# Placing batch 0's turning transfers behind the loads of the beginning, with a new load order and new deadlines

## The chip, the cores and the metric

The kernel runs on one core of one Trainium2 chip. The metric is the device time of one execution in microseconds (us). A core has five engines that each work through their own instructions in order: TensorE (PE in the profile; its weight loads are listed as PEld), VectorE (DVE), ScalarE (ACT), GpSimd (POOL) and SyncE (SP). SP issues every transfer (DMA) of this kernel, so its queue is the queue of all loads, turning transfers and stores. Engines wait for one another by semaphores.

## The reference, cut to what matters

There are B = 4 batches of S = 256 rows of H = 512 values. Four layers follow one another:

```python
# L0: a mixture of low-rank updates; ctx (4, 64, 512) plays the part of lora_A
w     = softmax(x @ router_W.T + router_b)            # (4, 256, 8)
a_sum = einsum('bsh,arh->bsr', x, ctx)               # sums over a, the batches of ctx
x     = nan_to_num(x + 0.5 * einsum('bsn,bsnh->bsh', w, einsum('bsr,nhr->bsnh', a_sum, lora_B)))
# L1: cross attention to ctx, 32 heads of 16, masked, then layer norm
Q, K, V = x @ Wq.T + bq, ctx @ Wk.T + bk, ctx @ Wv.T + bv
x     = layernorm(x + attention(Q, K, V, mask) @ Wo.T + bo) * ln_g + ln_b
# L2 and L3, the same function with the same weights: 4 blocks each
idx   = the 8 nearest of 512 columns of ctx[b] for each column (squared distance over 64 rows)
for i in range(4):
    p = leaky_relu(x)                                # x seen as (256, 512) per batch
    x = (f[i] @ p + sum over the 8 neighbours of f[i] @ p[:, idx]) / 9 + x
```

Each batch's chain goes through L0, L1 and then eight blocks, each of which needs the one before. The neighbour search depends on ctx alone and is needed only when the batch's first block begins.

## The kernel before, in words

For every batch the kernel builds the operations of `mixture` (L0; `mix` does it for each half of 128 rows), `values`, `queries` and `attention` (L1), `nearest` (the search) and eight times `block`. `keys`, `masks` and `lora_a` are made once for all batches.

**The search.** `nearest(b)` computes on PE four PSUM banks `dist` of negated half distances for batch b: `cross` (line 517) and the squares (line 530). For each bank j, DVE finds the eight largest values (`top`, line 537) and replaces them by a mark (`rest`, line 540), ACT makes zeros and ones of it (`near`, line 547, bf16), and POOL adds the identity (line 556). Then SP issues a DMA that transposes `near` into a quarter of the tile `turned` (line 566): this is what is called a turning transfer here, and there are four per batch. ACT last copies `turned` into the four `nbr` tiles of the batch (line 580), which the blocks multiply by on PE (line 920): there the sum over neighbours is a matmul.

**Batch 0's chain at the beginning.** `route` on PE (line 396), a small softmax on DVE and `z` (line 424), zT on PE (442) and its copy on ACT (447), `upd` on PE (452), x on DVE (467), then `hi` and `lo` (473, 474) on DVE, their sum on POOL (475), `odd` (476) and the predicated copy (477) on DVE, which are nan_to_num; then x1T on PE (481), its copy on ACT (487), and q on PE (690). Line 850 is the addition of attention's output to x, also on DVE.

**The planner.** No order is written out by hand. Every operation is added to a `Plan` with its engine, a cost in us, and the keys that it reads and writes. `emit` then simulates the engines: it always takes, for each engine, among the ready operations that could start first the one of lowest rank, and emits the earliest of these choices. So it fixes the order of the instructions on each engine, and the choice of tiles; it is no wait on the chip. The chip waits only for what the tiles demand: data, places, and a free DMA semaphore. An operation's rank is its batch's entry in `DEADLINES` less the costs behind it; a load's rank is its place in the list of loads, ahead of everything else. A load ends, for the planner, at the latest landing so far plus its size over `RATE` (0.3 MB per us), and at most `LANES` = 8 loads are under way:

```python
if op.load:
    op.end = max(op.end + 1.4, self.landed[-1]) + op.load / RATE
    self.landed.append(op.end)
op.end += op.lag
```

A turning transfer has no size: it costs SP the time `TURN` and lands `LAG` later by the planner's reckoning, whatever loads are under way.

**Places.** Tiles of a kind share a few places that the planner hands out: 8 PSUM banks, of which `stage` may hold 7 (blocks take a bank without `stage`), 5 of `half` (sq, rest, hi, lo, zTs, kT, seen and others), 5 of `near`, 4 of `full` (z, qT, turned, p), 3 of `xT` (xT and x1T). A tile can be written only when the operations on its place's last holder are done.

The functions that the diff touches:

Of the kernel before, what the change touches and what calls it, by code (L numbers as in the profile page):

```python
# [17 lines left out]
B, S, H = 4, 256, 512  # L18
# [10 lines left out]
SLOPE = 0.01  # L29
LN_EPS = 1e-5  # L30
LOW = -3.0e38
DEADLINES = (0.0, 2.0, 12.0, 17.0)

# [5 lines left out]
WARM = 20  # L41
LANES = 8
RATE = 0.3
TURN, LAG = 1.2, 1.2


class Buf:
# [121 lines left out]
def xattn_seq_kernel(ctx: ExitStack, tc: tile.TileContext, a: dict, out: bass.AP):  # L169
# [10 lines left out]
    shapes = {  # L180
        "bank": (psum, [128, 512], F32, 8),
        "xT": (keep, [128, NC, S], F32, 3),
        "s": (work, [128, H], F32, 8),
        "pT": (work, [128, H], F32, 4),
        "half": (work, [128, H], F32, 5),
        "full": (work, [128, 2, H], F32, 4),
        "wp": (work, [128, 2 * S], F32R, 8),
        "near": (work, [128, H], BF16, 5),
# [5 lines left out]
        pool, shape, dtype, _ = shapes[kind]  # L194
        return pool.tile(shape, dtype, tag=f"{kind}{place}", name=name)

    plan = Plan({kind: n for kind, (_, _, _, n) in shapes.items()} | {"stage": 7}, make)
    pe, act, dve, pool = (
        lambda *args, _e=e, **kw: plan.add(_e, *args, **kw) for e in ("PE", "ACT", "DVE", "POOL")
    )  # L200
# [9 lines left out]
    cxx = [keep.tile([128, H], F32, name=f"cxx{b}") for b in range(B)]  # L210
# [10 lines left out]
    rw = keep.tile([128, NC, NB + R], F32, name="rw")  # L221
    fT = keep.tile([128, NBLK, S // 128, S], F32, name="fT")
# [29 lines left out]
    def load(key, mb, dst, src, after=()):  # L252
        loads.append(key)
        plan.add("SP", 0.45, lambda: S_.dma_start(out=dst(), in_=src), after, (key,), rank=len(loads) - 1e4, load=mb)
# [4 lines left out]
    def load_xT(b):  # L259

        after = (("x1T", 1, 0),) if b == B - 1 else ()
        load(xT[b], 0.5, lambda: xT[b].tile.rearrange("p c t -> p (c t)"), a["xT"][b], after)

    def load_x(b):
        load(("x", b), 0.5, lambda: x1[b].rearrange("p l h -> p (l h)"), a["x"][b])

    def load_w(n):
        load(n, 1.0, lambda: w[n].rearrange("p c o -> p (c o)"), a[n])

    def load_k(o):  # L270
        load(("WkT", o), 0.25, lambda: WkT[o], a["WkT"][:, bass.ts(o, H)])

    def load_points(b):
        load(("cxx", b), 0.13, lambda: cxx[b][0:64], a["ctx"][b])
# [3 lines left out]
    load_k(0)  # L278
    load("ctxT", 0.5, lambda: ctxT.rearrange("p c b v -> p (c b v)"), a["ctxT"])
    load("small", 0.05, lambda: consts, a["small"])  # L280
    load_k(1)
    load_points(1)
    load_xT(0)
    load_w("lora_BT")
    load_k(3)
    load_points(2)
    load_x(0)
    load_k(2)
    load_points(3)
    load_w("WqT")  # L290
    load("mask_i", 0.12, lambda: mask_i.rearrange("p b v -> p (b v)"), a["mask"].partition_broadcast(128))
    load("rows1", 0.5, lambda: rows1, a["rows1"].partition_broadcast(128))
    load_w("WvT")
    load_xT(1)
    load("rows2", 0.5, lambda: rows2, a["rows2"].partition_broadcast(128))
    load_x(1)
    load_w("WoT")
    load_x(2)
    load("fT", 1.0, lambda: fT.rearrange("p i c o -> p (i c o)"), a["fsideT"])
    load_xT(2)  # L300


    dve(0.15, lambda: V_.memset(ones, 1.0), (), ("ones",))
# [192 lines left out]
    def nearest(b):  # L496
        sq = Buf("half", f"sq{b}")
        if b:
            act(0.6, lambda: A_.copy(cxx[b][64:128], cxx[b][0:64]), (("cxx", b),), (("cxx2", b),))
        act(0.6, lambda: A_.activation(sq.tile[0:64], cxx[b][0:64], AF.Square), (("cxx", b),), (sq,))  # L500
        act(0.6, lambda: A_.copy(csq[b][0:64], sq.tile[0:64]), (sq,), (("csq", b),))
        (pool if b else dve)(
            1.15 if b else 0.69,
            lambda: (G_ if b else V_).tensor_tensor(csq[b][64:128], sq.tile[0:64], csq[b][0:64].bitcast(F32), ALU.subtract),
            (sq, ("csq", b)),
            (("csq2", b),),
        )
        turned = Buf("full", f"turned{b}")
        dist = [Buf("bank", f"d2_{b}_{j}", "stage") for j in range(H // 128)]


        for k in range(2):

            def cross(k=k):
                for j in (2 * k, 2 * k + 1):
                    r = slice(64 * (j % 2), 64 * (j % 2) + 64)
                    T_.matmul(
                        dist[j].tile,
                        lhsT=cxx[b][r, bass.ts(j, 128)],
                        rhs=cxx[b][r],  # L520
                        start=True,
                        stop=False,
                        tile_position=(64 * (j % 2), 0),
                    )

            pe(0.9, cross, (("cxx", b), ("cxx2", b)), (dist[2 * k], dist[2 * k + 1], ("d2", b, k)))
            for j in (2 * k, 2 * k + 1):
                pe(
                    0.24,
                    lambda j=j: T_.matmul(dist[j].tile, lhsT=mhalf_r, rhs=csq[b], start=False, stop=True),  # L530
                    (("csq", b), ("csq2", b), "mhalf_r"),
                    (dist[j], ("d2", b, 2 + j)),
                )
        for j in range(H // 128):
            ps, top = dist[j], Buf("small", f"top{b}_{j}")
            rest, near = Buf("half", f"rest{b}_{j}"), Buf("near", f"near{b}_{j}")
            dve(0.69, lambda ps=ps, top=top: V_.max(top.tile[:, 0:KNN], ps.tile), (ps,), (top,))
            dve(
                0.76,
                lambda ps=ps, top=top, rest=rest: V_.match_replace(rest.tile, top.tile[:, 0:KNN], ps.tile, LOW),  # L540
                (ps, top),
                (rest,),
            )

            act(
                0.62,
                lambda rest=rest, near=near: A_.activation(
                    near.tile, rest.tile, AF.Relu, bias=above, scale=-(2.0**-123)
                ),
                (rest, "above"),  # L550
                (near,),
            )

            pool(
                0.3,
                lambda j=j, near=near: G_.tensor_tensor(
                    near.tile[:, bass.ts(j, 128)], near.tile[:, bass.ts(j, 128)], ident_h, ALU.add
                ),
                ("ident_h",),
                (near,),  # L560
            )

            plan.add(
                "SP",
                TURN,
                lambda j=j, near=near: S_.dma_start_transpose(
                    out=turned.tile.rearrange("p l h -> p (l h)").bitcast(BF16).rearrange("p (k n) -> p k n", k=4)[
                        :, :, bass.ts(j, 128)
                    ],
                    in_=near.tile,  # L570
                ),
                (near, turned),
                (("turned", b, j),),
                lag=LAG,
            )
        for k in range(H // 128):

            def store(k=k):
                nbr[b, k] = keep.tile([128, H], F32R, tag=nbr_tag[b][k], name=f"nbr{b}_{k}")
                A_.copy(  # L580
                    nbr[b, k],
                    turned.tile.rearrange("p l h -> p (l h)").bitcast(BF16)[:, bass.ts(k, H)],
                )


            gone = [("kT", o) for o in range(NC)] if b == 1 else []
            if b > 1:
                gone = [("d2", i, j) for i in (2 * b - 4, 2 * b - 3) for j in range(2 + H // 128)]
            act(0.6, store, (turned, *(("turned", b, j) for j in range(H // 128)), *gone), (("nbr", b, k),))
# [359 lines left out]
    for b in range(B):  # L949
        plan.batch = b  # L950
        if b == B - 1:
            load_xT(b)
            load_x(b)
        mixture(b)
        values(b)
        queries(b)
        nearest(b)
        for i in range(2 * NBLK):
            plan.unit = (b, i)
            block(b, i)  # L960
        plan.unit = None
    plan.emit(DEADLINES)

# [48 lines left out]
```

## Time and profile before

| what | us |
|---|---|
| median of three runs | 409.84 (409.74 to 410.01) |
| the profiled execution, its own time | 411.24 |
| its span, from the first to the last instruction | 408.9 |
| granted TensorE clock, mean | 0.994 of full |

The page divides the span into 40 equal slices of 10.2 us; each digit is the busy share of a slice in tenths:

```profile
PE   8996999999799999999999999999999999999995
DVE  4629669699889999873776554646455464635443
ACT  3823534335478574341223111111111111111110
DMA  6999410000020000000001000000000000010102
GB/s 200 353 349 334 105 52 2 0 2 2 0 53 2 0 2 2 0 2 0 2 0 26 2 0 0 2 0 2 0 1 2 0 0 2 0 51 2 51 0 103
```

The first four slices hold the loads. The first block begins at 145.8 us (line 889); from about 205 us on PE does nothing but blocks. A row of the timeline gives start, duration, engine, line, operation, tiles, shape and count, and in brackets the idle time of that engine before it and what ended it. In SP's timeline the first transfers that turn stand among the loads:

```profile
17.26 1.30 SPq L566 DMA_TRANSPOSE turned<-near  x1
18.61 0.57 SPq L254 DMA_DIRECT2D rows<-in_rows  x1
19.22 0.43 SPq L254 DMA_DIRECT2D x<-in_x  x1
20.71 0.33 SPq L254 DMA_DIRECT2D WoT<-in_WoT  x1
21.15 9.35 SPq L566 DMA_TRANSPOSE turned<-near  x3
30.55 0.57 SPq L254 DMA_DIRECT2D x<-in_x  x1
31.17 0.44 SPq L254 DMA_DIRECT2D fT<-in_fsideT  x1
31.71 1.38 SPq L566 DMA_TRANSPOSE turned<-near  x1
```

The four at 17.26 and 21.15 are batch 0's.

### The profile page before, as it was taken

The numbers are of one execution on the slowest core, as the hardware profiler recorded it, in microseconds if no ns is written. First come the engines' busy times: TensorE is split into PE (matmuls) and PEld (weight loads), VectorE is DVE, ScalarE is ACT, GpSimd is POOL, SyncE is SP. The second block draws the span as 40 slices with busy tenths as digits, with TensorE's granted clock in tenths as the row PEclk, the third lists the DMA queues.
The fourth block names the chain that finished last, engine by engine and source line by source line (L and its number), as shares of the span: only waits on it lengthen the run. The fifth ranks groups of instructions, "written<-read, shape, count | busy, mean of one in ns | idle before, by whom it ended". The sixth has DMA issues, their size and how long they took to land.

```text
span 408.9 us, 5691 instructions
## 1 busy us (share of the span) xinstructions
PE 394.7 (97%) x2244; PEld 302.9 (74%) x2244; DVE 266.0 (65%) x476; ACT 132.0 (32%) x236; POOL 100.3 (25%) x110
## 2 busy tenths in 40 slices
PE   8996999999799999999999999999999999999995
PEld 5753598646676686766878888888888888888884
DVE  4629669699889999873776554646455464635443
ACT  3823534335478574341223111111111111111110
POOL 4854240326736690950500000000000000000000
PEclk9999999999899999999999999999999999999999
DMA  6999410000020000000001000000000000010102
GB/s 200 353 349 334 105 52 2 0 2 2 0 53 2 0 2 2 0 2 0 2 0 26 2 0 0 2 0 2 0 1 2 0 0 2 0 51 2 51 0 103
DMA packets 13450, 17.42 MB, mean 43 GB/s; under 512 B 9392, under 2 KB 9520, under 8 KB 12784
## 3 DMA queue, kind: packets, MB, share of 16 engines
q1 hardware_dynamic: 13424, 17.07, 13.5%
q8 instruction: 17, 0.28, 0.3%
q14 instruction: 9, 0.07, 0.1%
HBM read 12.87 MB, written 2.10 MB: 37 GB/s over the span
## 4 chain that ended last, share of the span: by engine, by line
PE 76%; DVE 14%; DMA 4%; ACT 2%; POOL 2%; issue 1%; SPq 0%; DVEq 0%; ACTq 0%; POOLq 0%
PE blk L920 29%; PE wp L889 26%; PE q L690 6%; PE upd L452 5%; PE o L838 3%; DMA turned<-near 3%; PE pT L806 2%; DVE den L772 2%; PE s L731 1%; DVE x L477 1%; DMA ctxT<-in_ctxT 1%; DVE s L763 1%; DVE odd L476 1%; DVE mx L757 1%; DVE p L877 1%
## 5 line engine op out<-in xcount | busy, mean ns | idle before, releaser
L889 PE MATMUL wp<-fT,p 128*128 128x256 f32 x512 | 120.3, 379 | 0.0
L920 PE MATMUL blk<-nbr,wph 128*128 128x512 f32 x256 | 112.1, 438 | 0.0
L889 PEld LDWEIGHTS wp<-fT,p 128*128 128x128 f32 x512 | 96.5, 189 | 16.5 <-issue 1.4
L905 DVE TENSOR_TENSOR wpl<-wp,wph 128x512 fp32r<-128x512 f32 x64 | 44.2, 690 | 93.5 <-ACT wph L902 93.5
L920 PE MATMUL blk<-nbr,wpl 128*128 128x512 f32 x256 | 100.5, 392 | 0.1
L902 ACT CAST wph<-wp 128x512 fp32r<-128x512 f32 x64 | 37.5, 586 | 177.7 <-PE wp L889 177.7
L920 PEld LDWEIGHTS blk<-nbr,wph 128*128 128x128 f32 x256 | 48.2, 188 | 11.4 <-issue 1.2
L920 PEld LDWEIGHTS blk<-nbr,wpl 128*128 128x128 f32 x256 | 48.2, 188 | 10.3 <-DVE wpl L905 0.4
L932 DVE SCALAR_TENSOR_TENSOR x<-blk,x 128x512 f32<-128x512 f32 x64 | 42.6, 686 | 11.0 <-PE blk L920 11.0
L877 DVE SCALAR_TENSOR_TENSOR p<-x 128x512 f32<-128x512 f32 x64 | 44.9, 736 | 2.5 <-POOL x L864 1.9
L794 POOL TENSOR_TENSOR s<-s,rden 128x512 f32<-128x512 f32 x32 | 35.9, 1152 | 37.7 <-DVE rden L784 24.4
L690 PE MATMUL q<-x1T,WqT 128*128 128x256 f32 x128 | 30.8, 393 | 2.4 <-DVE x L850 2.4
L838 PE MATMUL o<-WoT,avTs 128*128 128x512 f32 x64 | 30.1, 600 | 0.5 <-ACT avTs L832 0.4
L690 PEld LDWEIGHTS q<-x1T,WqT 128*128 128x128 f32 x128 | 24.3, 195 | 6.8 <-DVE x L850 2.6
L452 PE MATMUL upd<-lora_BT,zTs 128*128 128x512 f32 x64 | 28.7, 595 | 0.0
L757 DVE TENSOR_REDUCE mx<-s 128x8 f32<-128x512 f32 x32 | 19.9, 682 | 7.7 <-PE s L731 7.7
L769 ACT ACTIVATE s<-s 128x512 f32<-128x512 f32 x32 | 18.8, 626 | 14.4 <-DVE s L763 14.4
L452 PEld LDWEIGHTS upd<-lora_BT,zTs 128*128 128x128 f32 x64 | 11.9, 190 | 12.8 <-issue 11.7
L772 DVE TENSOR_REDUCE den<-s 128x8 f32<-128x512 f32 x32 | 20.1, 675 | 0.8 <-ACT s L769 0.8
L811 ACT COPY pTs<-pT 128x512 f32<-128x512 f32 x32 | 17.2, 590 | 9.0 <-PE pT L806 9.0
L763 DVE TENSOR_TENSOR s<-s,mx 128x512 f32<-128x512 f32 x32 | 19.9, 679 | 0.0
L838 PEld LDWEIGHTS o<-WoT,avTs 128*128 128x128 f32 x64 | 11.4, 190 | 11.2 <-issue 9.7
(94 smaller groups left out, 370.5 us busy)
## 6 DMA issues: line engine op xcount, KB each, us to landing
xT<-in_xT SPq DMA_DIRECT2D x4, 512.0 KB, 7.1
x<-in_x SPq DMA_DIRECT2D x4, 512.0 KB, 7.9
out<-x SPq DMA_DIRECT2D x8, 256.0 KB, 2.0
WkT<-in_WkT SPq DMA_DIRECT2D x4, 256.0 KB, 7.3
lora_BT<-in_lora_BT SPq DMA_DIRECT2D x1, 1024.0 KB, 8.3
WqT<-in_WqT SPq DMA_DIRECT2D x1, 1024.0 KB, 10.8
rows<-in_rows SPq DMA_DIRECT2D x2, 512.0 KB, 10.0
WvT<-in_WvT SPq DMA_DIRECT2D x1, 1024.0 KB, 11.3
```

Source lines behind the costliest of these rows:

```text
L452: T_.matmul(ps2.tile, lhsT=zT.tile[:, bass.ts(c, 128)], rhs=w["lora_BT"][:, c, :], start=(c == 0), stop=(c == NC - 1),)
L690: T_.matmul(ps.tile[:, 0:S], lhsT=w["WqT"][:, c, bass.ts(o, 128)], rhs=x1T[b].tile[:, c, :], start=(c == 0), stop=(c == NC - 1),)
L757: lambda mx=mx, ps=ps: V_.tensor_reduce(mx.tile[:, 0:HPC], heads(ps), AX.X, ALU.max),
L772: lambda s=s, g=g: V_.tensor_reduce(den.tile[:, bass.ts(g, HPC)], heads(s), AX.X, ALU.add),
L794: lambda s=s, g=g: G_.tensor_tensor(heads(s), heads(s), rden.tile[:, bass.ts(g, HPC)].unsqueeze(2).to_broadcast([128, HPC, V]), ALU.mult,),
L838: T_.matmul(po.tile, lhsT=avT.tile[:, bass.ts(c, 128)], rhs=w["WoT"][:, c, :], start=(c == 0), stop=(c == NC - 1),)
L877: lambda l=l: V_.scalar_tensor_tensor(p.tile[:, l], pt[:, l], SLOPE, pt[:, l], ALU.mult, ALU.max),
L889: T_.matmul(ps.tile[:, bass.ts(k, S)], lhsT=p.tile[:, c, bass.ts(2 * m2 + k, 128)], rhs=wi[:, c, :], start=(c == 0), stop=(c == NL - 1),)
L902: act(0.59, lambda ps=ps, hi=hi: A_.copy(hi.tile, ps.tile), (ps,), (hi,))
L905: lambda ps=ps, hi=hi, lo=lo: V_.tensor_tensor(lo.tile, ps.tile, hi.tile.bitcast(F32), ALU.subtract),
L920: T_.matmul(pb[o].tile, lhsT=part.tile[:, bass.ds(m % 2 * S + o * 128, 128)], rhs=nbr[b, m], start=(m == 0 and k == 0), stop=(m == H // 12 ...
L932: lambda o=o: V_.scalar_tensor_tensor(pt[:, o], pb[o].tile, 1.0 / (KNN + 1.0), pt[:, o], ALU.mult, ALU.add),
```

## The change

It has five parts. A turning transfer now reads, besides its tiles, the keys `rw`, `fT` and x of batches 1 and 2, so that the planner places it after the operations that write these: the loads of fT, x1 and x2, and for `rw` an ACT copy of the router's weights (line 350). This stands in `nearest`, so it holds for every batch. The order of the loads is another. The deadlines of batches 2 and 3 are 5 us earlier. `stage` may hold all 8 banks. And three costs of the planner differ: `cross`, `TURN` and `LAG`. The instructions themselves, their number and their shapes stay as they are.

```diff
--- before.py
+++ after.py
@@ -29,7 +29,7 @@
 SLOPE = 0.01
 LN_EPS = 1e-5
 LOW = -3.0e38
-DEADLINES = (0.0, 2.0, 12.0, 17.0)
+DEADLINES = (0.0, 2.0, 7.0, 12.0)
 
 
 
@@ -41,7 +41,7 @@
 WARM = 20
 LANES = 8
 RATE = 0.3
-TURN, LAG = 1.2, 1.2
+TURN, LAG = 1.23, 1.6
 
 
 class Buf:
@@ -194,7 +194,7 @@
         pool, shape, dtype, _ = shapes[kind]
         return pool.tile(shape, dtype, tag=f"{kind}{place}", name=name)
 
-    plan = Plan({kind: n for kind, (_, _, _, n) in shapes.items()} | {"stage": 7}, make)
+    plan = Plan({kind: n for kind, (_, _, _, n) in shapes.items()} | {"stage": 8}, make)
     pe, act, dve, pool = (
         lambda *args, _e=e, **kw: plan.add(_e, *args, **kw) for e in ("PE", "ACT", "DVE", "POOL")
     )
@@ -278,26 +278,26 @@
     load_k(0)
     load("ctxT", 0.5, lambda: ctxT.rearrange("p c b v -> p (c b v)"), a["ctxT"])
     load("small", 0.05, lambda: consts, a["small"])
+    load_xT(0)
+    load_points(1)
     load_k(1)
-    load_points(1)
-    load_xT(0)
+    load_k(2)
     load_w("lora_BT")
+    load_x(0)
     load_k(3)
+    load_w("WqT")
+    load_points(3)
     load_points(2)
-    load_x(0)
-    load_k(2)
-    load_points(3)
-    load_w("WqT")
     load("mask_i", 0.12, lambda: mask_i.rearrange("p b v -> p (b v)"), a["mask"].partition_broadcast(128))
     load("rows1", 0.5, lambda: rows1, a["rows1"].partition_broadcast(128))
+    load_xT(1)
     load_w("WvT")
-    load_xT(1)
+    load_w("WoT")
+    load_x(1)
     load("rows2", 0.5, lambda: rows2, a["rows2"].partition_broadcast(128))
-    load_x(1)
-    load_w("WoT")
+    load_xT(2)
+    load("fT", 1.0, lambda: fT.rearrange("p i c o -> p (i c o)"), a["fsideT"])
     load_x(2)
-    load("fT", 1.0, lambda: fT.rearrange("p i c o -> p (i c o)"), a["fsideT"])
-    load_xT(2)
 
 
     dve(0.15, lambda: V_.memset(ones, 1.0), (), ("ones",))
@@ -506,6 +506,7 @@
             (("csq2", b),),
         )
         turned = Buf("full", f"turned{b}")
+        landed = ("rw", "fT", *(("x", k) for k in range(1, B - 1)))
         dist = [Buf("bank", f"d2_{b}_{j}", "stage") for j in range(H // 128)]
 
 
@@ -523,7 +524,7 @@
                         tile_position=(64 * (j % 2), 0),
                     )
 
-            pe(0.9, cross, (("cxx", b), ("cxx2", b)), (dist[2 * k], dist[2 * k + 1], ("d2", b, k)))
+            pe(1.1, cross, (("cxx", b), ("cxx2", b)), (dist[2 * k], dist[2 * k + 1], ("d2", b, k)))
             for j in (2 * k, 2 * k + 1):
                 pe(
                     0.24,
@@ -569,7 +570,7 @@
                     ],
                     in_=near.tile,
                 ),
-                (near, turned),
+                (near, turned, *landed),
                 (("turned", b, j),),
                 lag=LAG,
             )
```

## The prediction

> **What bounds the kernel now.** I read the page's totals first, then TensorE's (PE's) timeline and its waits, then the chain that ended last, and last the timelines of the engines that this chain names. All shares and times below are of the one profiled execution.
>
> ```profile
> span 408.9 us, 5691 instructions
> PE 394.7 (97%) x2244; PEld 302.9 (74%) x2244; DVE 266.0 (65%) x476; ACT 132.0 (32%) x236; POOL 100.3 (25%) x110
> ```
>
> PE is busy for 394.7 of 408.9 us, and the change alters no matmul, so 14.2 us of PE idleness is all there is to win. The last matmul ends at about 404.5; the 4.4 us behind it (the last x update on DVE and the store of the output) and 2.0 us at the start (1.1 for `ones`, 0.9 for ctxT) are not touched. What is left are these waits in PE's timeline (start, duration, instruction, and in brackets the idle time before it and its releaser):
>
> ```profile
> 36.62 0.66 PE L481 MATMUL x1T<-ident,x 128*128 128x128 f32 x4 [2.74 <-DVE x L477]
> 39.69 0.66 PE L481 MATMUL x1T<-ident,x 128*128 128x128 f32 x4 [1.13 <-DVE st L419]
> 41.50 1.06 PE L442 MATMUL zT<-ident,z 128*128 128x128 f32 x8 [0.69 <-DVE z L424]
> ...
> 106.36 3.10 PE L690 MATMUL q<-x1T,WqT 128*128 128x256 f32 x8 [2.41 <-DVE x L850]
> ```
>
> The first three sum to 4.56 us and lie between 33.9 and 41.5: PE has run out of work and waits for batch 0's x1 from DVE. Why DVE is late there is told by the chain of work that ended last (start, duration, what) and by ACT's and DVE's timelines:
>
> ```profile
> 17.26 10.71 DMA turned<-near
> ...
> 28.05 0.73 ACT near L547
> ...
> 29.89 0.70 DVE x L467
> ```
> ```profile
> 28.05 0.72 ACT L547 ACTIVATE near<-rest,above 128x512 bf16<-128x512 f32 x1 [5.24 <-DMA turned<-near]
> 34.49 2.18 ACT L580 CAST nbr<-turned 128x512 fp32r<-128x512 bf16 x4 [5.71 <-DMA turned<-near]
> ```
> ```profile
> 28.81 0.29 DVE L640 TENSOR_SCALAR seen<-mask_i 128x256 f32<-128x256 int32 x1 [6.60 <-ACT near L547]
> ```
>
> The first turning transfer of batch 0 is issued at 17.26 and lands 10.71 us later, while in the calm stretch after 37 us four of them land in 2.8 us in the median. There are 5 places for `near`. Four are batch 0's, the fifth is batch 1's first, and batch 1's second can be written only when that transfer has landed. It stands on ACT from 22.8 to 28.05; the `rest` tile that it has to read keeps a "half" place, which `seen` waits for on DVE, and the x update of batch 0 (L467) is queued behind `seen`. Its input, the first upd bank, was complete at about 24.4 (upd starts at 20.93, half of 7.03 us). The stretches show the same:
>
> ```profile
> 20.00:25.00 5.00, 5.00 (x16) 2.71 (x15) 1.01 (x4) 2.78 (x6) 4.82 (x6) 1.00 1.02 394
> 25.00:30.00 5.00, 5.00 (x25) 2.20 (x23) 1.09 (x5) 0.72 (x1) 0.85 (x2) 1.00 1.21 302
> 30.00:35.00 5.00, 3.88 (x34) 2.92 (x32) 4.79 (x12) 0.51 (x1) 1.72 (x2) 1.00 1.06 354
> 35.00:40.00 5.00, 2.25 (x12) 1.19 (x13) 4.82 (x10) 2.98 (x7) 2.66 (x3) 1.00 1.13 329
> ```
>
> Columns: stretch and length, busy time of PE, weight load, DVE, ACT, POOL, then granted clock, DMA share, GB/s. DVE works 2.1 of 10 us at 20 to 30, is then full, and PE starves behind it. DMA is saturated (share 1.0 and more) until about 40.
>
> **The change, part by part.**
>
> *Turning transfers behind the loads.* The new inputs rw, fT and x of batches 1 and 2 are only in the plan: the transfer gets no wait of its own on the chip, but the planner places it, on SP, after these loads have landed by its reckoning. Batch 0's four are moved past the loads of rows2, x1, WoT, x2 and fT that now stand behind or between them; those of batch 1 past xT2. When do they land? The loads of the beginning sum to 11.82 MB (from the page's KB); 200 GB/s in the first slice is 2.0 MB by 10 us, and the other 9.8 MB at 350 GB/s take 28, so about 38 us; with 2.8 for a turn, 40 to 41. By the planner's 0.3 MB/us the same loads end at about 39.5 and the turn at 42.3. So the plan is no longer too hopeful, and ACT and DVE get an order in which nothing of batch 0 stands behind a `near` without a place. On SP four issues of 1.26 us (median, L566) come behind the loads, where nobody waits: xT3 was issued at 52.9. Queued behind them on SP are x3, xT3 and batch 1's turns. The five `near` places stay taken until about 40, so three of batch 1's four searches (0.61 for the maxima, 0.76 for the replacement, 1.37 us each, 4.1 together) move from 19 to 45 us to later. Batch 0's nbr is first read at 152.0, so 100 us hide its delay.
>
> What then sets x1T of batch 0? upd's first bank at 24.4, DVE x 0.69, hi, lo, odd 1.2, POOL 1.3, copy_predicated 0.7 to 1.8 (it ran 1.79 beside POOL): 28.5 to 29.5. The second bank, at 27.9, leads to 32 to 33. PE has other work until 33.9 (v of two batches, route of batch 1), so x1T no longer waits, and 6.9 us of q follow, in which z of batch 1 is finished. The whole 4.56 goes. Bounds: 0 if another wait fills it, 4.56 if not; I take 4.56, since every duration is from a row and 0.9 us of slack is left. If that cover is gone (WvT late, so that v comes late), up to 1.95 us of v per batch is missing; by bytes WvT lands at about 25 to 26, as it did (14.78 + 11.3 = 26.1).
>
> *Order of loads.* WkT's second piece moves behind xT0 and points 1, 640 KB, or 2 us at 300 to 350 GB/s: it landed at about 9.1 (from 3.62) and now at about 11. xT0 moves ahead by 384 KB, from 11.0 to about 9.9. PE finishes the first piece of kT at 9.95 and can go on with route of batch 0 only when POOL's rw is there at 10.37: 0.4 us of idle; if the order keeps kT first, 1.2. I take 0.45 as a loss. Behind it PE is full up to 34, so a gain in z's readiness is worth nothing by itself. lora_BT lands 0.7 us later than its 13.55, long before 20.9. x0, WqT, mask and rows1 keep their place within 0.6 MB. All hidden.
>
> *Stage 7 to 8, cross 0.9 to 1.1, TURN and LAG.* No instruction and no duration; only the order. 7 or 8 banks: between -1 and +1 us, taken as 0, as no PE wait of before comes from a missing bank.
>
> *Deadlines of batches 2 and 3, 5 us earlier.* Ranks only, among operations that are ready together. They touch 45 to 205 us, where DVE is at 9 to 10 of 10 for long stretches (80 to 110, 120 to 170). The trace can't show it. Bounds: it may close the 2.41 us gap at 103.9, or open another like it. **A rule to weigh:** "TensorE: Matmul & The Clock Gate" in the Trainium skill (part 1, the HAM clock gate) has the clock halved only after an idle window of about 3.4 us. The row here is harsher: after 2.41 us of idleness the clock is halved for three microseconds.
>
> ```profile
> 107.00:108.00 1.00, 1.00 (x5) 0.79 (x4) 1.00 (x2) 0.00 (x0) 0.00 (x0) 0.55 0.00 0
> 108.00:109.00 1.00, 1.00 (x4) 0.82 (x3) 0.95 (x5) 0.78 (x3) 0.00 (x0) 0.50 0.00 0
> ```
>
> In the chain the eight q matmuls there take 3.10 instead of 1.73 and eight pT 1.45 instead of 0.87, 1.95 more. The gaps at 34 to 41 ran at a granted 1.00. So this gap is worth 2.41 by the rule, 4.36 by the row, and a new one costs its length by the rule and up to 1.95 more by the row. I count by the row, and take 0 in the likeliest case, between -4.4 and +5.
>
> *Sum.* 411.24 (profiled execution: span 408.9 and 2.34 around it) - 4.56 + 0.45 = 407.1. The median of the runs is 1.40 below the profiled execution, so **405.7 us**.
>
> **The rivals.**
> (B) Both gaps close: 405.7 - 4.36 = 401.3. For it: DVE's idle 7.9 us at 20 to 30 are partly regained, so it is less behind later. Against: DVE waits for PE at 45 to 80 anyway (idle for 10.3 us), so what it regains early need not reach 103.
> (C) The 4.1 us of batch 1's searches land in the full stretch of DVE before 104: the gap there grows by as much, and nothing is gained but the half clock lasts longer: 405.7 + 4.1 + 0 to 1.95, so 409.8 to 411.8. For it: DVE is at 9.2 to 10 of 10 from 80 on. Against: 5.6 us of DVE idleness at 45 to 60 can take them.
> (D) Slower outright: **the "half" places**. There are five. While `near` has no place until 40, `rest` tiles of batch 1 computed at 20 may hold three of them, and hi and lo of batch 0 need two beside zTs. If hi or lo gets none before the turns land, batch 0's copies stand as before, only behind 40 instead of 28: x1T goes from 36.6 to as late as 48, up to 11.5 us, 413 to 421. It decides from the point where ACT's sixth `near` stands ahead of batch 0's x1T copies. Against: the planner reckons with these places, and late turns now.
> (E) The stall stays in part, as the turns land later than planned and ACT waits at L547 or L580 again, 2 to 3 us: 408 to 409.5.
>
> **How the numbers follow.** The likeliest case (first gap closed, the rest as before) gets 0.42, own range 404.0 to 407.5; B 0.13, C 0.25, D 0.12, E 0.08. A difference under 0.2% (0.8 us) can't be told from none. Faster: all of the first two, 0.04 of C, 0.05 of E, together 0.64; same: 0.06 of C, 0.03 of E, 0.09; slower: 0.15 of C and D, 0.27. The range from 401.5 to 413.5 leaves out most of D and the lower part of B, under 0.2.
>
> **What would show it.** Right: turned<-near first on SP after 25 us and behind fT; no ACT wait of several us for it before 45; x1T's first wait on PE under 0.5 us; PE's busy time 394 to 395 in a span near 404.8. C would show as a longer wait of q or pT near 100 and a granted clock of 0.5 after it; D as ACT near or DVE hi waiting until 40. Wrong would make it above all the part that no row shows: what the new ranks do between 45 and 205 us.

## The result, and the profile after

The changed kernel takes **404.87 us** in the median of 4 runs (403.52 to 405.6), the kernel before beside it 409.92. The recorded ratio is 0.9865 (the medians alone give 0.9877), with a 95% interval of 0.9827 to 0.9903. A second set of 6 runs on another occasion gave 404.14 us and 0.9846 (0.9817 to 0.9874). The forecast was 405.7, in a range of 401.5 to 413.5. No execution of the changed kernel in either set (at most 405.61) took as long as the quickest of the kernel before in any set (406.38).

The totals of the page of the changed kernel, which was profiled in an execution of 405.6 us:

```profile
span 403.9 us, 5708 instructions
PE 393.7 (97%) x2244; PEld 303.3 (75%) x2244; DVE 266.4 (66%) x476; ACT 128.8 (32%) x234; POOL 100.7 (25%) x110
```

The four stretches of 20 to 40 us, with the columns of the prediction (length, PE, weight load, DVE, ACT, POOL, clock, DMA share, GB/s):

```profile
20.00:25.00 5.00, 5.00 (x12) 2.21 (x13) 1.26 (x5) 3.06 (x6) 0.93 (x2) 1.00 1.04 347
25.00:30.00 5.00, 5.00 (x28) 3.81 (x27) 4.29 (x11) 0.71 (x2) 3.40 (x3) 1.00 0.99 409
30.00:35.00 5.00, 5.00 (x44) 3.27 (x43) 4.87 (x10) 0.72 (x2) 3.08 (x3) 1.00 1.02 417
35.00:40.00 5.00, 5.00 (x23) 3.02 (x23) 2.49 (x6) 2.12 (x4) 1.70 (x2) 1.00 1.37 231
```

PE is now busy in all of them, where it lost 3.87 us in the last two before. DVE's work of 25 to 30 has gone from 1.09 to 4.29 us: batch 0's x is no longer held up. The first update of x begins at 25.28 instead of 29.89, as DVE's timeline has it, and ACT reads the first transfers without any wait (no bracket behind the second line):

```profile
25.28 0.69 DVE L467 SCALAR_TENSOR_TENSOR x<-upd,x 128x512 f32<-128x512 f32 x1 [1.40 <-PE upd L452]
```
```profile
48.10 2.16 ACT L581 CAST nbr<-turned 128x512 fp32r<-128x512 bf16 x4
```

SP's timeline shows the transfers issued behind the last loads:

```profile
23.72 2.48 SPq L254 DMA_DIRECT2D x<-in_x  x2
28.43 25.33 SPq L567 DMA_TRANSPOSE turned<-near  x6
```

Batch 0's four landed at 40.38 to 42.60, just after the last of these loads (39.75), and 5.5 us ahead of the nbr copies. What PE does meanwhile is read from the chain that ended last (start, duration, what):

```profile
34.08 1.02 PE zT L442 x8
35.10 0.23 PE d L531
35.34 0.44 PE x1T L481 x4
35.77 3.44 PE upd L452 x8
39.21 1.74 PE route L396 x16
40.95 3.48 PE upd L452 x8
44.43 0.44 PE x1T L481 x4
```

PE goes on with upd of batch 1 and route of batch 2 before batch 0's second x1T. DVE had both halves of batch 0's x ready by 35.18, so it is PE's order that puts the second one so late. The waits that PE has left, apart from the start, lie elsewhere:

```profile
138.48 1.08 PE L819 MATMUL avT<-pTs,vbd 128*32 128x128 f32 x32 [0.49 <-ACT pTs L812]
140.42 1.66 PE L807 MATMUL pT<-ident,s 128*128 128x128 f32 x12 [0.86 <-DVE s L764]
142.90 0.63 PE L807 MATMUL pT<-ident,s 128*128 128x128 f32 x4 [0.81 <-ACT pTs L812]
158.62 1.56 PE L890 MATMUL wp<-fT,p 128*128 128x256 f32 x6 [0.93 <-DVE p L878]
```

They sum to 3.09 us and are new. The wait of 2.41 us at 103.9 is gone, and so is the halved TensorE clock (half clock) behind it.

The account of the two profiled executions: the last matmul ends at 398.1 instead of 404.6, 6.4 us earlier. Of this, 5.4 are idleness of PE up to there (9.86 to 4.44 us) and 1.0 its busy time (394.7 to 393.7). Gone are 4.56 (the first waits), 2.41 (the wait at 103.9), 0.90 (ctxT), 0.43 (a wait for avTs at 132) and, in the busy time, 1.95 (the half clock). New are the 3.09 at 138 to 160, 0.24 for cxx, and 1.40 of slower matmuls at the very start. That is 5.5; the other 0.9 are gaps and stretched matmuls too small to name. Behind the last matmul the changed kernel loses 1.4 again, since the last store landed after 3.5 us instead of 2.0. So the span is 5.0 shorter.

### The profile page after: what moved, and what is told of

It is laid out like the page before. It is cut to its first block, busy times and chain, and to the rows that moved or that the text cites. A ratio compares the mean times of both kernels' runs of the same rounds, so it can differ in the third digit from the quotient of the medians.

```text
span 403.9 us, 5708 instructions
## 1 busy us (share of the span) xinstructions
PE 393.7 (97%) x2244; PEld 303.3 (75%) x2244; DVE 266.4 (66%) x476; ACT 128.8 (32%) x234; POOL 100.7 (25%) x110
## 4 chain that ended last, share of the span: by engine, by line
PE 94%; DVE 3%; ACT 1%; DMA 1%; issue 1%; ACTq 0%; DVEq 0%
PE blk L921 29%; PE wp L890 27%; PE q L691 7%; PE upd L452 7%; PE o L839 7%; PE pT L807 3%; PE d L518 2%; PE kT L599 2%; PE route L396 2%; PE s L732 2%; PE avT L819 2%; PE v L653 1%; PE d L531 1%; PE zT L442 1%; PE x1T L481 1%; DVE p L878 1%
## 5 line engine op out<-in xcount | busy, mean ns | idle before, releaser
L878 DVE SCALAR_TENSOR_TENSOR p<-x 128x512 f32<-128x512 f32 x64 | 45.9, 756 | 2.8 <-PE wp L890 2.1
L795 POOL TENSOR_TENSOR s<-s,rden 128x512 f32<-128x512 f32 x32 | 32.7, 1055 | 33.8 <-DVE rden L785 33.8
L691 PE MATMUL q<-x1T,WqT 128*128 128x256 f32 x128 | 29.6, 383 | 0.0
L773 DVE TENSOR_REDUCE den<-s 128x8 f32<-128x512 f32 x32 | 19.8, 678 | 0.8 <-ACT s L770 0.8
L839 PEld LDWEIGHTS o<-WoT,avTs 128*128 128x128 f32 x64 | 11.6, 190 | 11.5 <-issue 11.3
L758 DVE TENSOR_REDUCE mx<-s 128x8 f32<-128x512 f32 x32 | 19.8, 683 | 0.2 <-PE s L732 0.2
## 6 DMA issues: line engine op xcount, KB each, us to landing
rows<-in_rows SPq DMA_DIRECT2D x2, 512.0 KB, 11.5
```

What stands on the lines that cost most here:

```text
L691: T_.matmul(ps.tile[:, 0:S], lhsT=w["WqT"][:, c, bass.ts(o, 128)], rhs=x1T[b].tile[:, c, :], start=(c == 0), stop=(c == NC - 1),)
L758: lambda mx=mx, ps=ps: V_.tensor_reduce(mx.tile[:, 0:HPC], heads(ps), AX.X, ALU.max),
L795: lambda s=s, g=g: G_.tensor_tensor(heads(s), heads(s), rden.tile[:, bass.ts(g, HPC)].unsqueeze(2).to_broadcast([128, HPC, V]), ALU.mult,),
L839: T_.matmul(po.tile, lhsT=avT.tile[:, bass.ts(c, 128)], rhs=w["WoT"][:, c, :], start=(c == 0), stop=(c == NC - 1),)
L878: lambda l=l: V_.scalar_tensor_tensor(p.tile[:, l], pt[:, l], SLOPE, pt[:, l], ALU.mult, ALU.max),
```

## Experiments

### 1. Undo the titular part, keep the order of work

The titular part is the new inputs of the turning transfers, which place them behind the loads.

```diff
-        landed = ("rw", "fT", *(("x", k) for k in range(1, B - 1)))
...
-                (near, turned, *landed),
+                (near, turned),
```

> The changed kernel without its titular part: the turning transfers get no new inputs, so batch 0's stand among the loads again; the orders of PE, DVE and POOL are the changed kernel's to the last instruction, ACT's differs only in where batch 0's four nbr copies stand (behind sq and csq of batches 2 and 3, ahead of the second lg). Theory M (a late turning transfer blocks ACT): the nbr copies wait on ACT until the fourth transfer lands at 29 to 31 us, lg and z of batch 1 come 3 to 4 us late, PE waits 2 to 4 us between 30 and 40, 407 to 408.5 us. Rival O (the gain is that of the new orders of loads and work, the place of the transfers has nothing to do with it): 404 to 405.7 us, no wait on PE above 1 us before 45.

Measured: 411.77 us, ratio to before 1.0036 (1.0016 to 1.0056), so the whole gain is gone. ACT's and PE's timelines and two stretches of 1 us:

```profile
32.88 2.18 ACT L580 CAST nbr<-turned 128x512 fp32r<-128x512 bf16 x4 [9.27 <-DMA turned<-near]
```
```profile
38.46 1.94 PE L442 MATMUL zT<-ident,z 128*128 128x128 f32 x8 [4.57 <-DVE z L424]
```
```profile
38.00:39.00 1.00, 0.54 (x3) 0.57 (x4) 0.99 (x3) 0.00 (x0) 1.00 (x2) 0.55 0.84 344
39.00:40.00 1.00, 1.00 (x7) 1.00 (x6) 0.99 (x3) 0.36 (x1) 1.00 (x2) 0.50 0.99 393
```

ACT stands for 9.27 us at the nbr copies; behind them in its queue are lg (at 36.24 instead of 29.71) and with it z of batch 1, and PE waits 4.57 us. The changed kernel's waits at 138 to 160 come again, 6.4 us later, each the same within 0.01 us. PE, DVE and POOL have the same order in both; ACT's differs only in the four nbr copies, SP's only in the four transfers. So rival O falls here: an ACT that stands at a reader of a late transfer is the cause. PE's last matmul ends at 404.5, 6.4 us later than in the changed kernel: 4.7 of it are waits and 1.6 busy time. So the half clock is a part of why it cost more than was expected.

### 2. The titular part alone

```diff
+        landed = ("rw", "fT", *(("x", k) for k in range(1, B - 1)))
...
-                (near, turned),
+                (near, turned, *landed),
```

> The kernel before with the titular part alone. Theory M: ACT no longer waits for turned<-near before 45 us and PE's waits at 34 to 41 (4.56 us) are gone; the total is then 405.5 if the rest of the order is as good as before's, and up to 411 if the planner, with loads and deadlines not searched anew, makes gaps between 70 and 115. Rival O: the waits at 34 to 41 stay or move by a few us, 409 to 411.

Measured: 418.99 us, ratio 1.0225 (1.0161 to 1.029). PE's waits in its timeline:

```profile
37.54 1.07 PE L442 MATMUL zT<-ident,z 128*128 128x128 f32 x8 [0.56 <-DVE z L424]
91.19 1.11 PE L481 MATMUL x1T<-ident,x 128*128 128x128 f32 x4 [3.97 <-DVE x L477]
...
94.43 3.52 PE L691 MATMUL q<-x1T,WqT 128*128 128x256 f32 x8 [0.68 <-ACT x1T L487]
...
101.87 3.06 PE L807 MATMUL pT<-ident,s 128*128 128x128 f32 x12 [3.49 <-DVE rest L541]
```

The 4.56 us are down to 0.56, and ACT does not wait for a turning transfer before 45: this part of the theory holds. But DVE is full between 85 and 105 (19.8 of 20 us), PE waits there for 8.5 us, and runs the eight q matmuls in 3.52 us, at a granted clock of 0.50. The time was expected at up to 411; it is 8 us more. It looks like rival C of the prediction, a DVE that is late near 100, but C's reason does not hold: the searches (tile top) take DVE 8.26 us between 15 and 45, as long as in the kernel before (8.29), so they were not pushed out of the beginning. In the changed kernel they were, as forecast (2.00 us there), and 5.94 us of them lie between 85 and 105 without any wait on PE.

### 3. More places for near, in the order of before

```diff
+        if kind == "near":
+            place = len(handed) % 8
+            handed.append(name)
```

> The kernel before with every instruction in its order, but near tiles laid on 8 places in turn instead of 5, so that ACT's sixth near needs no landed transfer. Theory M: the ACT wait of 5.24 us for near is gone and DVE's seen comes at about 23 instead of 28.8, but the second wait, nbr for batch 0's transfers until 34.5, stands ahead of the x1T copies, which come at 37 to 38; PE's waits shrink from 4.56 to 3 to 4 us, 408.5 to 409.5 us. If the near place alone is the cause: 405.3. Rival O: 409.8, nothing changes.

Measured: ratio 1.0008 (0.9976 to 1.004), no difference. ACT's sixth near comes at 22.72, no longer waiting. Then:

```profile
36.43 2.17 ACT L585 CAST nbr<-turned 128x512 fp32r<-128x512 bf16 x4 [12.99 <-DMA turned<-near]
```
```profile
42.38 1.94 PE L447 MATMUL zT<-ident,z 128*128 128x128 f32 x8 [5.71 <-DVE z L429]
```

The wait for a place is replaced by the next instruction in ACT's queue that needs the same transfers. PE waits 5.71 us instead of 4.56. The size can't be compared: this execution took 414.21 us, where the median of the 20 is 411.38, and the fourth transfer landed at 36.36 in it, 1.9 us later than in the profile of the kernel before. But the wait is there, and the time of the runs shows no gain: the sixth near was not the cause by itself, the lateness of the transfers to an engine in order was. I had expected a shrinking to 3 or 4.

### 4. Tell the planner a later landing, leave the transfers where they are

```diff
-                lag=LAG,
+                lag=LAG if b else 11.0,
```

> The kernel before, in which only the planner's landing time of batch 0's transfers is put from 1.2 to 11 us (what the trace shows); they stay among the loads on SP. If it is enough that the planner knows how late they land (a part of theory M): no ACT wait for them above 1 us, PE's 4.56 us are gone, 405 to 406 us. If the place behind the loads is what matters (they hold up the loads, or land later still): 409 to 410. Rival O: 409 to 411, since loads and deadlines are the old ones.

Measured: 417.39 us, ratio 1.0149 (1.0065 to 1.0234), slower than either case. ACT, DVE, PE, and a piece of the chain that ended last:

```profile
35.81 0.72 ACT L547 ACTIVATE near<-rest,above 128x512 bf16<-128x512 f32 x1 [12.21 <-DMA turned<-near]
```
```profile
36.56 0.43 DVE L473 TENSOR_SCALAR hi<-x 128x512 f32<-128x512 f32 x1 [7.00 <-ACT near L547]
```
```profile
40.80 1.09 PE L481 MATMUL x1T<-ident,x 128*128 128x128 f32 x4 [8.17 <-DVE x L477]
```
```profile
28.54 7.16 DMA turned<-near
```

The near waits 12 us and hi of batch 0 for a half place behind it: the mechanism of rival D, at a price of 8.17 us of idleness. The transfer that was waited for is the fifth turning transfer on SP, batch 1's first, issued at 28.54 and landed at 35.70. The edit left batch 1's landing time at 1.2 us (`LAG if b else 11.0`), and in the planner's order batch 1's second near takes the place of its first, which the planner believes free soonest. Batch 0's four had all landed by 35.05. So the planner was told of one late landing and not of the next, and the experiment does not answer whether knowledge is enough. The next one comes nearer.

### 5. Transfers early on SP, their readers late on ACT

Against the changed kernel, in addition to the edit of experiment 1:

```diff
-                lag=LAG,
+                lag=LAG if b else 22.0,
```

> The changed kernel with batch 0's transfers among the loads on SP again (first after 14 us, as in the run without the titular part), but with the planner told that they land 22 us later, so that ACT's nbr copies stand behind lg, zTs and x1T of batch 0 and the orders of PE and DVE stay the changed kernel's. If only the place of the readers on ACT matters: no ACT wait for turned<-near above 1 us, no PE wait above 1 us before 45, 404 to 406 us. If the transfers' place on SP matters too (they hold up the loads behind them): 407 to 411, with PE waiting for WvT, xT or x of batches 0 and 1.

Measured: 405.43 us, ratio 0.9856 (0.9815 to 0.9898), the changed kernel's time. SP's, ACT's and PE's timelines:

```profile
15.08 2.67 SPq L566 DMA_TRANSPOSE turned<-near  x2
```
```profile
42.87 2.18 ACT L580 CAST nbr<-turned 128x512 fp32r<-128x512 bf16 x4
```
```profile
27.84 1.98 PE L396 MATMUL route<-rw,xT 128*128 128x72 f32 x16 [1.26 <-DMA xT<-in_xT]
```

The transfers stand among the loads from 15 us on and hold xT of batch 1 up by 1.26 us on PE, and yet the gain is there. PE and DVE have the same order as in experiment 1, and the four transfers stand at nearly the same places on SP. What separates the two is, near enough, the place of four copies on ACT: 6.3 us. The place of the transfers on SP is worth about a microsecond: this is the one wait that they add on PE.

### 6, 7, 8 and 12. The other parts, each put back alone

```diff
-DEADLINES = (0.0, 2.0, 7.0, 12.0)
+DEADLINES = (0.0, 2.0, 12.0, 17.0)
```

> The changed kernel with the deadlines of before (12 and 17 for batches 2 and 3). My prediction counted the deadlines at nothing, between -4.4 and +5: then 404 to 406 us. If the new deadlines are what keeps DVE's full stretch from starving PE (rival C held off by the search): new PE waits between 80 and 150 of 5 us and more in sum, some with half the clock behind them, 411 to 417.

Experiment 7 puts back the block of loads:

```diff
+    load_k(1)
+    load_points(1)
     load_xT(0)
-    load_points(1)
...
```

> The changed kernel with the load order of before. If the order of loads matters only by which data is late (my prediction: all hidden, 0.45 us lost): 404 to 405.5. If the planner's order of work turns with it: waits at other places, between 95 and 172, of 3 to 5 us in sum, 408 to 412. The waits before 45 stay away in both, since the transfers stay behind the loads.

Experiment 8:

```diff
-TURN, LAG = 1.23, 1.6
+TURN, LAG = 1.2, 1.2
...
-            pe(1.1, cross, (("cxx", b), ("cxx2", b)), (dist[2 * k], dist[2 * k + 1], ("d2", b, k)))
+            pe(0.9, cross, (("cxx", b), ("cxx2", b)), (dist[2 * k], dist[2 * k + 1], ("d2", b, k)))
```

> The changed kernel with the three old costs of the planner (cross 0.9, turning 1.2 and 1.2). My prediction: these cost nothing by themselves, -1 to +1, so 404 to 406. If the planner's choice hangs on every hundredth (its order is a draw, and the search picked this one): many waits from 88 to 170, over 10 us in sum, 416 to 424.

Experiment 12:

```diff
-    plan = Plan({kind: n for kind, (_, _, _, n) in shapes.items()} | {"stage": 8}, make)
+    plan = Plan({kind: n for kind, (_, _, _, n) in shapes.items()} | {"stage": 7}, make)
```

> The changed kernel with 7 banks for staged tiles as before. My prediction counted this at nothing, -1 to +1: 404 to 406. If the order turns with it as with the other parameters: a new wait near 130 of about 5 us with half the clock behind it, 411 to 414.

| put back | us | ratio to before (95%) |
|---|---|---|
| nothing (changed kernel, second set) | 404.14 | 0.9846 (0.9817 to 0.9874) |
| deadlines | 418.20 | 1.0167 (1.0125 to 1.0209) |
| load order | 407.24 | 0.9900 (0.9859 to 0.9941) |
| costs | 422.25 | 1.0264 (1.0214 to 1.0314) |
| stage | 409.65 | 0.9974 (0.9963 to 0.9986) |

With the old deadlines PE's busy time on the page is 400.7 us, 7.0 more than the changed kernel's with the same matmuls, and the longest of its waits is

```profile
101.73 1.08 PE L481 MATMUL x1T<-ident,x 128*128 128x128 f32 x4 [4.37 <-DVE x L477]
```

With the old costs:

```profile
98.73 9.82 PE L691 MATMUL q<-x1T,WqT 128*128 128x256 f32 x32 [4.19 <-DVE s L764]
```

(32 such matmuls take 7.17 in the changed kernel), and with stage 7:

```profile
129.80 3.04 PE L839 MATMUL o<-WoT,avTs 128*128 128x512 f32 x4 [2.27 <-DVE vbd L671]
```

All four make a longer time, by 3 to 18 us against the second set, and no wait for batch 0's transfers comes back. For the load order the intervals overlap a little, though its four runs (406.88 to 407.47) all lie above the ten of the changed kernel. The four differ from one another by which engine PE waits for, and when, between 85 and 182. The three costs change no instruction, and putting them back costs 18 us. The bank costs 5.5, with a wait of 2.27 us near 130 where about 5 was expected. In each of the four the orders on PE, DVE, ACT and POOL are others than the changed kernel's, so these are the prices of whole orders and not of single parts.

### 9, 10 and 11. The changed kernel again, and two further orders

Experiment 9 has no edit.

> The changed kernel itself, for the comparison with the next two on the same chip, and to see what of its profile is chance. If the 4.41 us of the first eight cross matmuls (3.01 before) and the 3.5 us landing of the last store (2.0 before) belong to the one execution, they differ here and the span is 402 to 403; if they belong to the order, they come again and the span is 403.9. The time 404 to 406.

Experiment 10, its core (the loads after small stand in another order too):

```diff
-DEADLINES = (0.0, 2.0, 7.0, 12.0)
+DEADLINES = (0.0, 2.0, 5.5, 11.5)
...
-TURN, LAG = 1.23, 1.6
+TURN, LAG = 1.23, 2.0
...
-            pe(1.1, cross, (("cxx", b), ("cxx2", b)), (dist[2 * k], dist[2 * k + 1], ("d2", b, k)))
+            pe(0.9, cross, (("cxx", b), ("cxx2", b)), (dist[2 * k], dist[2 * k + 1], ("d2", b, k)))
```

> The changed kernel with load order, deadlines (0, 2, 5.5, 11.5), LAG 2.0 and cross 0.9 from a further search, in which an order was judged by how it runs when transfers land as late as the traces show and every cost is a few per cent off. If the waits left at 138 to 160 (3.1 us) can be searched away without opening the first gap again: 401 to 403.5. If orders are a draw beyond what such a search can foresee: 404 to 410.

Experiment 11 differs likewise: deadlines (0, 2.5, 6, 11.5), RATE 0.34, LAG 1.8, cross 1.05, another order of loads.

> A second order from the same search, with deadlines (0, 2.5, 6, 11.5), RATE 0.34, LAG 1.8 and cross 1.05, and batch 1's xT and the mask ahead of lora_BT. The same two cases: 401.5 to 404, or 404 to 410; where it loses, the waits lie before 45 (lora_BT or x of batch 0 too late) rather than at 138 to 160.

Measured: 404.14 us for the changed kernel (403.97 to 405.61), **402.91** for the first order (402.7 to 404.13; ratio to before 0.9821, 0.9794 to 0.9848), 403.98 for the second (403.65 to 405.73). The first order is 1.2 us below the changed kernel in the median, but the intervals overlap. Its longest waits after the start are 2.33 and 0.32 us, for avTs. The span of the changed kernel came again as 403.9, with the slow matmuls at the start and the late last store. Whether these belong to its order the first eight cross matmuls of three kernels tell, in the order repeated changed kernel, search a, before with 8 near places:

```profile
3.41 4.41 PE L518 MATMUL d<-cxx 64*128 64x512 f32 x8
```
```profile
3.35 2.98 PE L518 MATMUL d<-cxx 64*128 64x512 f32 x8
```
```profile
3.35 4.30 PE L522 MATMUL d<-cxx 64*128 64x512 f32 x8
```

The last has the instruction order of the kernel before, whose own profile shows 3.01; experiment 6 has the changed kernel's order up to here, and shows 3.44. So one order gives both, and about 1.4 us at the start are chance of the execution; search a's profile had the lucky side of it. Up to the last matmul the profiles of search a and of the repeated changed kernel differ by about as much, 1.36 us. How much of the 1.2 us between the medians it is stays open. The store's 3.5 us came in both profiles of the changed kernel and in one other kernel (3.7, experiment 4), and 2.0 to 2.1 elsewhere; its cause was not sought.

## Why the prediction was right, and where it was not

**The first waits: right.** They were to vanish whole, 4.56 us, and none of them is left. Undoing the titular part brings a wait of 4.57 back at the same stretch and the whole gain with it.

**The mechanism: right in kind, wrong in what matters of it.** The prediction said that the transfers, moved behind the loads, would land when the planner expects them, and ACT and DVE would get an order that fits. The forecast of the landings was good (40 to 41; they came at 40.4 to 42.6). That readers must stand late in the order is shown by experiments 1 and 5. That the transfers must stand late is not needed: with them early on SP the time is the same, as long as ACT's readers stand late. It also named the sixth near and its place as the root; experiment 3 gives it a place, and the nbr copies, which it had listed as ACT's second wait, take over with nothing gained.

**x1T of batch 0: wrong in its times.** Its data were to be ready by 32 to 33, with q next on PE. They are ready at 35.18; the first half is turned at 35.34, the second at 44.43. PE did not wait, because upd of batch 1 and route of batch 2 fill the time. The cover was other work than the one named.

**Order of loads, 0.45 us lost: not seen.** Experiment 6, with the same loads and quick cross matmuls, waits 0.93 us for ctxT (0.90 before), and route follows without a wait. Put back alone, the old load order costs 3.1 us, through the order of work later on and not through late data.

**The deadlines, stage and costs: the step that failed.** They were taken as 0, with bounds of -4.4 to +5 for the deadlines, -1 to +1 for the banks, and none for the costs. Put back alone they cost 14, 5.5 and 18 us. The sum came out because the order that all parts make together closed the gap at 103.9 with its half clock, 4.36 us as in rival B, and opened only 3.09 us at 138 to 160. Experiment 1 has the same waits there and no gap at 103.9, so this is not the titular part's doing. With the slow start (1.40) and the late store (1.4) in the profiled execution this more than cancels, and the total falls next to the likeliest case. The hit at 0.8 us is in part luck.

**Rivals.** Both gaps of B closed, but others opened. C's searches did move into the stretch near 100, and PE did not wait for it; the late DVE of experiment 2 has another reason, which was not sought. D's wait of hi for a place was seen in experiment 4. E did not come.

**The clock.** The prediction counted by the row and not by the rule it weighed. Shorter gaps than that rule's bear this out: one of 2.27 us (experiment 12) and one of 2.32 (experiment 11) have a granted 0.50 behind them. But one of 2.33 (experiment 10) and the 2.74 before 36.6 in the kernel before left it at 1.00, so the length of a gap does not decide. What does is in the recorded clock. In each trace the stretches between two changes of the clock are whole multiples of 3.41 us long (3.41, 6.83, 30.7, 102.4 and more), so the changes lie on a grid. In the kernel before the gap of 2.74 falls into two cells of its grid, and the gap of 2.41 into one:

```profile
35.42:38.83 3.41, 1.95 (x9) 0.88 (x9) 3.30 (x7) 2.56 (x6) 2.02 (x3) 1.00 1.20 318
103.69:107.10 3.41, 1.00 (x6) 0.71 (x5) 3.41 (x5) 0.00 (x0) 3.14 (x3) 1.00 0.00 0
107.10:110.51 3.41, 3.41 (x12) 2.84 (x11) 3.29 (x11) 1.84 (x5) 0.72 (x1) 0.50 0.00 0
```

With PE busy for 1.95 us of a cell the clock stays; with 1.00 the next cell has half of it. Over the 14 traces, all 14 cells at full clock in which PE stood for 2.00 us or more were followed by half the clock, and none of the 1587 in which it stood for at most 1.63. In the changed kernel no such cell has more than 1.18 us (1.35 when repeated), so its waits of 3.09 us cost their length alone. The grid lies elsewhere in each execution (the full clock is first recorded at 9.28 us in the changed kernel and at 7.40 in its repetition), so whether a gap of 2.4 us costs 1.95 us more is partly chance.

## What to carry to other kernels

Where an engine works in order, a transfer costs not by where it is issued but by which instructions stand behind its first reader; look for the reader's place in the queue first, and check the next reader before adding a buffer for one. A planner that believes a transfer lands at once writes such readers too early, and no wait of the plan shows it; only the trace does. Where an order is found by search, a parameter put back alone says nothing on its worth in another order, and the gain of a part is to be measured with the search's choice around it. A gap on PE of 2 to 3 us has no fixed price here: look whether it falls into one cell of the clock's grid.

## What the runs showed of the hardware

TensorE's clock changed only on a grid of 3.41 us, and was halved after each cell in which PE stood for 2.00 us or more, and after none with at most 1.63 (14 traces). The first eight cross matmuls took 2.98 to 3.44 us in 8 of the 14 profiles and 4.19 to 4.46 in the other 6, with the same instructions at nearly the same time. In the 8 the full clock is first recorded at 4.6 to 5.7 us, in the 6 at 7.3 to 9.3; ahead of that no clock is recorded, and the 1.00 in the rows means no more than this. A turning transfer of 128 by 512 bf16 landed after 2.4 us with no load under way and after up to 13.9 among loads (12.3 in the kernel before). Copy_predicated took 0.67 to 0.74 us with no POOL operation beside it and up to 1.8 where one had begun about 0.1 us before it; where POOL's began 0.16 us after it (49.70 in the changed kernel), it took 0.73 and POOL's addition 1.66 instead of 1.27.
